# A selective scan on one core: a quarter of the B products of seven groups in twelve go from VectorE to ScalarE and TensorE, and GpSimd works on two units at a time

## The chip, the cores and the metric

The kernel runs on one core of a Trainium2 chip. The metric is device time in microseconds (us). The kernel before took 11069.99 us, the median of three runs (11064.06 to 11072.44).

## What is computed

The input is `x` of 8 x 96 x 64 x 64. A state-space block (layer norm, an in-projection, a depthwise convolution, a selective scan in four directions, a gate, an out-projection), then a convolution block with channel attention, linear attention and a small feed-forward layer with rounded 8-bit weights. The scan matters here. For each of 8 images, 4 directions (`K`) and 192 channels (`d`), with 16 states (`n`) and 4096 places:

```python
def step(h, inp):
    u_t, d_t, b_t, c_t = inp
    dA = jnp.exp(d_t[..., None] * A)
    h = dA * h + (d_t * u_t)[..., None] * b_t[:, :, None, :]
    y = jnp.einsum('bkdn,bkn->bkd', h, c_t)
    return (h, y)
```

So for every channel and state there are a decay `dA`, a product of delta x with B, a first-order recurrence, a product with C, and a sum over states.

## The kernel before

**Units.** Images are taken in pairs `p`. The 192 channels of two images make three tiles `T` of 128 rows: `T` 0 and 1 are the first 128 channels of the one and of the other image, `T` 2 holds the last 64 of both. The 4096 places are cut into four chunks of 1024. A *job* is one (pair, direction, chunk, tile), 192 in all; the tiles of a chunk come in the order 0, 2, 1. A job has four *groups* `j` of 32 channels, and a group four *units* `q`, each of 32 channels x 4 states on 128 partitions x 1024 places. That makes 768 groups and 3072 units.

**The work of a unit.** `spread` (L1299): TensorE copies 32 rows of delta x to all 128 partitions in `pu`, two PSUM banks, by a matmul with a 0/1 matrix, once for a group. `scan` (L1311) handles two units, a *pair*: VectorE multiplies `pu` by the broadcast B rows `bm` into `pb0` and `pb1` (two banks each), then runs the two recurrences (`tensor_tensor_scan`) out of `da` and `pb` into `hc`; GpSimd copies the last column of each unit into `carry` for the next chunk, and multiplies `hc` by the broadcast C rows `cm`. `decay` (L1304): ScalarE makes `da`, the exponential of delta times A, four buffers deep. `total` (L1349): TensorE adds the 4 x 4 states of a group into `yp` with 16 small matmuls; for directions 2 and 3 an identity matmul puts the earlier direction's sum (`prev`) there first, and for direction 2 of all pairs but the first another one (`yet`). ScalarE then copies `yp` to `y`. `hc` has eight buffers (L426), two groups deep.

**Order.** Each engine executes its instructions in the order in which the program records them (`InOrder`, L263 on); nothing overtakes. The main loop (L1400 on) records for every pair: `slots.run()`, `scan`, DMAs for B and C rows, the `decay` of the next pair, at the second pair of group g also `spread(g + 1)` and then `total(g - 1)`, and again `slots.run()`. The ScalarE copy of `yp` is recorded in that last `slots.run()`.

**Background.** Everything else (convolutions, norms, gates, the later layers of earlier pairs, and `steps`, L467, which prepares delta and delta x of the next job) is cut into small pieces, and each `slots.run()` records a few. `Slots` (L283) hands them two PSUM banks, `pg` and the bank of `yp`, and limits them by a budget of TensorE and ScalarE time: it refills by `RATE` and saves up to `CAP`, and each piece pays its estimated time.

Of the kernel before, what the change touches and what calls it, by code (L numbers as in the profile page):

```python
# [25 lines left out]
R = 6  # L26
# [255 lines left out]

class Slots:  # L283
# [7 lines left out]
    RATE, CAP = (2.0, 1.8), (3.0, 2.4)  # L291

    def __init__(self, *banks):
        self.lanes, self.later, self.first, self.at, self.due = [], [], None, 0, {}
        self.banks, self.held, self.big = banks, set(), set()
        self.left, self.behind = [0.0, 0.0], lambda: False
# [3 lines left out]

    def take(self, pe, act, long=0):
        while True:
            i = 1 if self.at % 2 and not long else 0


            due = long and (
                self.at % 4 > (long == 2) or self.at % 16 <= 6 < self.at % 16 + long
            )
            if i not in self.held and not due and min(self.left) > (-2 if long else 0):
                self.held.add(i)  # L310
                self.pay(pe, act)
                return self.banks[i]
            yield
# [7 lines left out]
    def give(self, bank):  # L321
        i = self.banks.index(bank)
        self.after(1, lambda: self.held.remove(i))
# [4 lines left out]
    def run(self):  # L328
        self.at += 1
        self.left = [min(v + r, c) for v, r, c in zip(self.left, self.RATE, self.CAP)]  # L330
        for f in self.due.pop(self.at, ()):
            f()
        if self.first is not None and next(self.first, self) is self:
            self.first = None
        order = [self.lanes, self.later]
        for lanes in order[::-1] if self.behind() else order:
            turn = self.at % len(lanes) if lanes else 0
            for lane in lanes[turn:] + lanes[:turn]:
                if next(lane, self) is self:
                    lanes.remove(lane)  # L340

    def idle(self):
        return not (self.lanes or self.later or self.first or self.due)
# [7 lines left out]
def phase_b(  # L351
# [8 lines left out]
    with ExitStack() as ctx:  # L360
# [28 lines left out]
        gmean = cp.tile([C, C], F32, name="gmean")  # L389
        nc.vector.memset(gmean, 1.0 / (C * 128))  # L390
# [35 lines left out]
        hp = inner.enter_context(tc.tile_pool(name="b_h", bufs=8))  # L426
# [23 lines left out]
        carries, bcs, dus, dls, sts, das, hcs, prevs, yet = ({} for _ in range(9))  # L450
# [11 lines left out]

        def exps():
# [3 lines left out]
        def steps(job):  # L467

            p, k, ci, c, T, at = where(job)
            if T == 0:  # L470

                sts[job // 3] = gp.tile([32 + 2 * R, 512], F32, name="st")
                r0 = 64 + R * (k // 2)
                for i, hs in enumerate(halves):
                    for b in range(2):
                        nc.sync.dma_start(
                            sts[job // 3][32 * i + R * b : 32 * i + R * b + R, :],
                            xd_d[k % 2][2 * p + b][r0 : r0 + R, at][:, hs],
                        )
# [5 lines left out]
            yield  # L485

            while slots.at % 16 != 6:
                yield
            dl = gp.tile([128, CH], F32, name="dls")
            for i, hs in enumerate(halves):  # L490
                bank = slots.banks[i]
                assert i not in slots.held
                slots.held.add(i)
# [11 lines left out]
            nc.sync.dma_start(dl_d[k][p][T][:, at], dl)  # L505
            yield

# [242 lines left out]
        def rest(b, s):  # L750
# [139 lines left out]
            for j in range(8):  # L890
# [17 lines left out]
                h8 = gp.tile([128, 3, 512], F8, name=f"h8{s}")  # L908
# [4 lines left out]
                for i in range(3):  # L913
                    bank = yield from slots.take(0.3, 1.3)
                    pe.matmul(bank, w1q[:, i * 128 : i * 128 + 128], x8, start=True, stop=True)
                    h16 = gp.tile([128, 512], F16, name=f"h16{s}")
# [11 lines left out]
                o16 = gp.tile([128, 512], F16, name=f"h16{s}")[0:C, :]  # L928
# [88 lines left out]
        def before_scans(p):  # L1017
# [26 lines left out]
            def norms(b):  # L1044
# [16 lines left out]
                for j in js:  # L1061
# [16 lines left out]
                    pe.matmul(bank[0:C, 0:4], gmean, cs, start=True, stop=True)  # L1078
                    se.mul(ngm, bank[0:C, 0:4], -1.0)
# [9 lines left out]
                    pe.matmul(bank[0:C, 0:4], gmean, gs, start=True, stop=True)  # L1089
                    se.activation(r, bank[0:C, 0:4], AF.Ln, bias=eps[0:C])  # L1090
# [177 lines left out]
        def weights(u, i):  # L1268
# [6 lines left out]
            if (job // 3, b, q, i) in bcs:  # L1275
                return
            t = bcp.tile([128, CH], F32, name=("bm", "cm")[i], bufs=(4, 5)[i])
            r0 = 32 * (k // 2) + 16 * i + 4 * q
            nc.sync.dma_start(
                t, xd_d[k % 2][2 * p + b][r0 : r0 + 4, at].unsqueeze(0).to_broadcast([32, 4, CH])  # L1280
# [30 lines left out]
        def scan(u):  # L1311
# [3 lines left out]
            step, last = (-1, 0) if k >= 2 else (1, CH - 1)  # L1315
            for i in range(2):
                ve.tensor_mul(pbs[i], pu, bcs[job // 3, batch(u), q + i, 0])
            for i in range(2):
                t = hp.tile([128, CH], F32, name="hc")
                carry = carries[p, k][:, T, 4 * j + q + i : 4 * j + q + i + 1]  # L1320
                ve.tensor_tensor_scan(
                    t[:, ::step], das.pop(u + i)[:, ::step], (pbs[i])[:, ::step],
                    0.0 if ci == 0 else carry, ALU.mult, ALU.add,
                )
                hcs[u + i] = t
            for i in range(2):
                v = u + i
                carry = carries[p, k][:, T, 4 * j + q + i : 4 * j + q + i + 1]
                if ci < NCH - 1:
                    ge.tensor_copy(carry, hcs[v][:, last : last + 1])  # L1330
                ge.tensor_mul(hcs[v], hcs[v], bcs[job // 3, batch(u), q + i, 1])
# [17 lines left out]
        def total(g):  # L1349
# [9 lines left out]
            for n in range(4):  # L1359
                for i in range(4):  # L1360
                    pe.matmul(
                        yp[32 * i : 32 * i + 32, :], add,
                        hcs[4 * g + n][:, 256 * i : 256 * i + 256],
                        start=(n == 0 and k < 2), stop=(n == 3),
                    )
            for n in range(4):
# [33 lines left out]
        for u in range(0, n, 2):  # L1400
# [37 lines left out]
            if q == 2:  # L1438
                if g + 1 < n // 4:
                    spread(g + 1)  # L1440
                if g > 0:
# [505 lines left out]
```

## Time and profile before

| | |
|---|---|
| median of the runs | 11069.99 us |
| the profiled execution, its span | 11058.4 us (the runs are 11.6 us longer at the median) |
| first scan starts, last scan ends | 222 us, 10724 us after the span's start |
| VectorE, GpSimd, TensorE, ScalarE busy | 95%, 82%, 71%, 60% of the span |
| mean granted TensorE clock | 0.815 of full |
| DMA | 1834 MB, 52.8% of 16 engines' span |

The profile is of one execution. "Idle before" a group of instructions is time in which its engine stood still just ahead of them, and the name behind the arrow is what ended it. A float32 matmul appears as two rows, a transpose by the identity as one. `x2` in a timeline merges neighbours of one kind, and its duration is from the start of the first to the end of the last. In names, `pb<-pu,bm` is written and read tiles. Nearly all of the scan's instructions have the line L266, the helper that records them.

### The profile page before, as it was taken

To read this page: it belongs to the slowest core of one execution; us is meant where nothing else is said; L and a number is where in the kernel's file an instruction comes from. 1 tells how busy PE (TensorE), PEld (TensorE's weight loads), DVE (VectorE), ACT (ScalarE), POOL (GpSimd) and SP (SyncE) were. 2 spreads that over 40 slices of the span, in tenths; PEclk is the share of its full clock that TensorE was granted. 3 is DMA by queue.
4 is the path that set the end of the run, shared out by engine and by line. 5 is a ranking of instruction groups with operands and counts; after the bars stand their busy time and mean duration, and the time that the engine had idled before them with its cause. 6 is when DMAs were issued, how large, how long until landed. Compare 5 with 4: busy or idle time off the path is not lost.

```text
span 11058.4 us, 128094 instructions
## 1 busy us (share of the span) xinstructions
PE 7887.2 (71%) x39468; PEld 3111.6 (28%) x39468; DVE 10525.7 (95%) x6651; ACT 6596.3 (60%) x9175; POOL 9028.7 (82%) x6649
## 2 busy tenths in 40 slices
PE   7755778655568887767777787776767776665778
PEld 3322333222223332223222332223322222222223
DVE  4999999999999999999999999999999999999974
ACT  2544765544567666556776656565776656665554
POOL 2788877787898888998888887899889888988860
PEclk8877888877788888878878888887878877777889
DMA  3445554454555555666545555566544555644551
GB/s 117 151 165 180 160 156 157 141 188 156 163 185 172 171 172 157 211 214 195 158 152 160 157 178 159 177 220 209 172 157 159 160 164 179 197 157 140 173 157 37
DMA packets 900188, 1834.20 MB, mean 166 GB/s; under 512 B 247965, under 2 KB 421214, under 8 KB 892462
## 3 DMA queue, kind: packets, MB, share of 16 engines
q1 hardware_dynamic: 899502, 1826.01, 52.8%
q8 instruction: 314, 5.14, 0.2%
q14 instruction: 372, 3.05, 0.1%
HBM read 1405.13 MB, written 420.42 MB: 165 GB/s over the span
## 4 chain that ended last, share of the span: by engine, by line
PE 32%; issue 29%; DVE 17%; POOL 11%; ACT 6%; DMA 4%; SPq 0%; DVEq 0%; POOLq 0%; ACTq 0%
PE pu L266 12%; PE yp L266 11%; DVE hc L266 11%; POOL hc L266 7%; PE pg L266 6%; DVE pb L266 5%; ACT u L266 2%; ACT da L266 2%; POOL u L266 2%; PE t L266 2%; PE ps L197 1%; DMA bm<-xd 1%; POOL turn L266 1%; POOL carry L266 1%; ACT L266 1%
## 5 line engine op out<-in xcount | busy, mean ns | idle before, releaser
L266 POOL TENSOR_TENSOR hc<-hc,cm 128x1024 f32<-128x1024 f32 x3072 | 7230.0, 2359 | 591.0 <-DVE hc L266 382.6
L266 DVE TENSOR_TENSOR_SCAN hc<-da,carry,pb 128x1024 f32<-128x1024 f32 x2304 | 5276.8, 2334 | 38.1 <-ACT da L266 31.5
L266 PE MATMUL pu<-du,c_sel 128*128 128x512 f32 x3072 | 2452.5, 944 | 2244.1 <-DVE pb L266 2239.6
L266 DVE TENSOR_TENSOR pb<-pu,bm 128x1024 f32<-128x1024 f32 x3072 | 3601.6, 1220 | 133.9 <-PE pu L266 105.9
L266 ACT ACTIVATE da<-dl,c_alog 128x1024 f32<-128x1024 f32 x3072 | 3352.8, 1140 | 91.4 <-DVE hc L266 73.8
L266 PEld LDWEIGHTS pu<-du,c_sel 128*128 128x128 f32 x3072 | 790.0, 281 | 3521.1 <-DVE pb L266 2784.8
L266 DVE TENSOR_TENSOR_SCAN hc<-da,pb 128x1024 f32<-128x1024 f32 x768 | 1713.1, 2275 | 38.9 <-ACT da L266 22.8
L266 ACT COPY y<-yp 128x256 f32<-128x256 f32 x768 | 284.4, 370 | 2348.9 <-PE yp L266 2198.4
L266 PE MATMUL yp<-hc,c_add 128*32 128x256 f32 x24576 | 1660.8, 416 | 22.6 <-ACT s L266 6.6
L266 PEld LDWEIGHTS yp<-hc,c_add 128*32 128x32 f32 x24576 | 768.6, 120 | 1200.1 <-issue 628.4
L266 POOL COPY carry<-hc 128x1 f32<-128x1 f32 x2304 | 422.5, 183 | 766.1 <-DVE hc L266 744.9
L266 ACT ACT_TABLE_LOAD x566 | 726.2, 1283 | 38.2 <-DMA cb<-zs 16.9
L266 ACT COPY u<-pg 128x512 f32<-128x512 f32 (+6 forms) x397 | 218.3, 550 | 712.3 <-PE pg L266 641.2
L266 POOL TENSOR_TENSOR u<-u,u 96x512 f32<-96x512 f32 (+1 forms) x426 | 537.5, 1269 | 105.9 <-ACT u L266 101.8
L266 POOL TENSOR_TENSOR du<-du,dls 128x1024 f32<-128x1024 f32 x192 | 452.7, 2358 | 91.5 <-ACT dls L266 91.1
L266 ACT COPY u<-yp 96x512 f32<-96x512 f32 (+6 forms) x347 | 188.0, 542 | 465.5 <-PE yp L266 404.5
L266 PE MATMUL pg<-ain,wmain 96*128 96x512 f32 x792 | 354.1, 599 | 0.0
L266 PE MATMUL pg<-ain,wmix 96*128 96x512 f32 x792 | 353.0, 598 | 0.0
L266 PE MATMUL yp<-prev,ident 128*128 128x256 f32 x768 | 321.9, 512 | 39.0 <-ACT u L266 27.4
L266 PEld LDWEIGHTS yp<-prev,ident 128*128 128x128 f32 x768 | 214.5, 283 | 381.8 <-issue 264.3
L266 PE MATMUL pg<-st,dtw 12*128 12x512 f32 x384 | 218.5, 649 | 49.4 <-ACT u L266 28.8
L266 PE MATMUL yp<-st,dtw 12*128 12x512 f32 x384 | 227.9, 674 | 18.3 <-ACT u L266 10.9
(340 smaller groups left out, 7030.2 us busy)
## 6 DMA issues: line engine op xcount, KB each, us to landing
dl<-dl SPq DMA_DIRECT2D x768, 512.0 KB
bm<-xd SPq DMA_DIRECT2D x512, 512.0 KB
cm<-xd SPq DMA_DIRECT2D x512, 512.0 KB
du<-xi SPq DMA_DIRECT2D x192, 512.0 KB
dl<-dls SPq DMA_DIRECT2D x192, 512.0 KB
ya<-y SPq DMA_DIRECT2D x384, 128.0 KB
prev<-ya SPq DMA_DIRECT2D x384, 128.0 KB
xi<-u SPq DMA_DIRECT2D x152, 256.0 KB
```

What stands on the lines that cost most here:

```text
L197: nc.tensor.matmul(bank[r, :].rearrange("p (h w) -> p h w", w=W), w[:, t if len(which) > 1 or w is wmix else 0, columns], pads[b][:, 8 * j ...
L266: op(*args, **kw)
```

## The change

For the first unit (`q` 0) of a group of tiles 0 and 1, save the first group of tile 0 in each chunk, VectorE's product of `pu` and `bm` is left out. That is 7 of a chunk's 12 groups, called *woven* here. Instead:

- `steps` loads four rows of B more for each image (four more DMAs of 8 KB a chunk), TensorE transposes them (8 transposes a chunk), ScalarE copies them to `bt`.
- `spin`, once for each job of tiles 0 and 1: TensorE transposes delta x (8 blocks of 128 x 128), ScalarE copies them to `dt` (2 copies of 128 x 512), then ScalarE multiplies each of the 8 blocks by each of 4 states' column of `bt`: 32 multiplications of 128 x 128, in four turns of eight, which write every fourth element of `t`. `spin` pays 2.4 for a turn.
- `weave(g + 1)`, recorded between `spread(g + 1)` and `total(g - 1)`: TensorE turns 8 blocks of `t` back into `pb0`.

GpSimd's carry copy and C product take both units of a pair in one instruction (128 x 2 and 128 x 2048), so `hc` becomes four double buffers in place of eight, and `cm` two double buffers in place of five. The budget's `RATE` and `CAP` rise from (2.0, 1.8), (3.0, 2.4) to (2.2, 2.0), (4.0, 4.0); a piece takes whichever of the two banks has rested longer. `dls`, `dt` and `t` share seven buffers; some other tiles share buffers, and a constant is dropped, to make room.

The core of the diff:

```diff
-    RATE, CAP = (2.0, 1.8), (3.0, 2.4)
+    RATE, CAP = (2.2, 2.0), (4.0, 4.0)
...
-            i = 1 if self.at % 2 and not long else 0
...
+            elif min(self.left) > 0:
+                free = [i for i in range(2) if i not in self.held and not (i == 1 and at % 4 == 0)]
+                if free:
+                    i = min(free, key=lambda i: self.used[i])
...
-        hp = inner.enter_context(tc.tile_pool(name="b_h", bufs=8))
+        hp = inner.enter_context(tc.tile_pool(name="b_h", bufs=4))
...
+        def weaves(u):
+            job, j, q = units[u]
+            return q == 0 and woven(job) and not (j == 0 and jobs[job][3] == 0)
...
+        def spin(job):
+            turns[job], b = [], jobs[job][3]
+            bt = bts[job // 3]
+            dt = gp.tile([128, 8, 128], F32, name="turned", bufs=RING)
+            for i in range(2):
+                bank = yield from slots.take(0.6, 0.6)
+                for x in range(4):
+                    pe.transpose(
+                        bank[:, 128 * x : 128 * x + 128],
+                        dus[job][:, 512 * i + 128 * x : 512 * i + 128 * x + 128],
+                        ident,
+                    )
+                se.copy(dt[:, 4 * i : 4 * i + 4, :], bank)
+                slots.give(bank)
+                yield
+            nxt = slots.at
+            while len(turns[job]) < 4:
+                n, at = len(turns[job]), slots.at % 16
+                if slots.at < nxt or (job and woven(job - 1) and n >= EXTRA and 3 < at < 12):
+                    yield
+                    continue
+                nxt = slots.at + 2 - b
+                slots.pay(0.0, 2.4)
+                t = gp.tile([128, 2, 128, 4], F32, name="turned", bufs=RING)
+                for i in range(2):
+                    for m in range(4):
+                        x, c = 2 * n + i, 4 * b + m
+                        se.mul(t[:, i, :, m], dt[:, x, :], bt[:, x, c : c + 1])
+                turns[job].append(t)
+                yield
+        def weave(g):
+            job, j, _ = units[4 * g]
+            for x in range(8):
+                t = turns[job][x // 2][:, x % 2].rearrange("p c n -> p (c n)")
+                pe.transpose(
+                    pbs[0][:, 128 * x : 128 * x + 128], t[:, 128 * j : 128 * j + 128], ident
+                )
...
             for i in range(2):
-                ve.tensor_mul(pbs[i], pu, bcs[job // 3, batch(u), q + i, 0])
+                if not weaves(u + i):
+                    ve.tensor_mul(pbs[i], pu, bcs[job // 3, batch(u), q + i, 0])
             for i in range(2):
...
-            for i in range(2):
-                v = u + i
-                carry = carries[p, k][:, T, 4 * j + q + i : 4 * j + q + i + 1]
-                if ci < NCH - 1:
-                    ge.tensor_copy(carry, hcs[v][:, last : last + 1])
-                ge.tensor_mul(hcs[v], hcs[v], bcs[job // 3, batch(u), q + i, 1])
+            if ci < NCH - 1:
+                ge.tensor_copy(carry, t[:, :, last])
+            ge.tensor_mul(t, t, bcs[job // 3, batch(u), q, 1])
...
                 if g + 1 < n // 4:
                     spread(g + 1)
+                    if weaves(4 * g + 4):
+                        weave(g + 1)
                 if g > 0:
                     total(g - 1)
```

## The prediction

> **What bounds the kernel now.** First the page's busy times and costliest groups:
>
> ```profile
> PE 7887.2 (71%) x39468; PEld 3111.6 (28%) x39468; DVE 10525.7 (95%) x6651; ACT 6596.3 (60%) x9175; POOL 9028.7 (82%) x6649
> ...
> L266 POOL TENSOR_TENSOR hc<-hc,cm 128x1024 f32<-128x1024 f32 x3072 | 7230.0, 2359 | 591.0 <-DVE hc L266 382.6
> L266 DVE TENSOR_TENSOR_SCAN hc<-da,carry,pb 128x1024 f32<-128x1024 f32 x2304 | 5276.8, 2334 | 38.1 <-ACT da L266 31.5
> ...
> L266 DVE TENSOR_TENSOR pb<-pu,bm 128x1024 f32<-128x1024 f32 x3072 | 3601.6, 1220 | 133.9 <-PE pu L266 105.9
> ```
>
> VectorE is busy for 95% of the span; its products and scans hardly wait. So the loop is VectorE's until something else is late. Second, the waits by engine, to see who stands close behind it:
>
> ```profile
> PE pu L266 <- DVE pb L266: 2239.6, 581, 14.5
> ACT y L266 <- PE yp L266: 2198.4, 670, 8.8
> ...
> DVE pb L266 <- PE pu L266: 105.9, 45, 20.4
> ...
> DVE hc L266 <- ACT da L266: 54.3, 43, 5.2
> ```
>
> TensorE comes early to `spread` in 581 of 768 groups, by 3.9 us each (2239.6/581). ScalarE stands at the copy of `yp` until TensorE has summed, 3.3 us each. Both hide their work behind VectorE, but each waits for the other once a group. Third, the timeline of one group and the next (direction 2, where `total` is longest), TensorE's and VectorE's lines:
>
> ```profile
> 5003.50 4.57 DVE L266 TENSOR_TENSOR_SCAN hc<-da,carry,pb 128x1024 f32<-128x1024 f32 x2
> ...
> 5003.65 3.78 PE L266 MATMUL pu<-du,c_sel 128*128 128x512 f32 x4 [2.45 <-DVE pb L266]
> ...
> 5007.99 2.34 DVE L266 TENSOR_TENSOR pb<-pu,bm 128x1024 f32<-128x1024 f32 x2
> ...
> 5008.53 1.93 PE L266 MATMUL yp<-hc,c_add 128*32 128x256 f32 x32
> ...
> 5010.24 4.58 DVE L266 TENSOR_TENSOR_SCAN hc<-da,carry,pb 128x1024 f32<-128x1024 f32 x2
> ...
> 5016.98 4.57 DVE L266 TENSOR_TENSOR_SCAN hc<-da,carry,pb 128x1024 f32<-128x1024 f32 x2
> ...
> 5017.12 1.98 PE L266 MATMUL pu<-du,c_sel 128*128 128x512 f32 x4 [1.19 <-DVE pb L266]
> ...
> 5019.90 1.93 PE L266 MATMUL yp<-hc,c_add 128*32 128x256 f32 x32
> ...
> 5021.47 2.34 DVE L266 TENSOR_TENSOR pb<-pu,bm 128x1024 f32<-128x1024 f32 x2
> ...
> 5023.71 4.58 DVE L266 TENSOR_TENSOR_SCAN hc<-da,carry,pb 128x1024 f32<-128x1024 f32 x2
> ```
>
> A pair takes VectorE 6.74 us (5003.50 to 5010.24), a group 13.48. The same `spread` takes 3.78 us in one group and 1.98 in the next; the mean clock is 0.815. Its rows have 944 ns in the mean, between 590 (fast) and 1222 (slow): (944-590)/(1222-590), some 0.56 of `spread` is slow.
>
> **Part 1: the products removed.** 7 groups of 12, 64 chunks (4 pairs x 4 directions x 4), one product each: 448. Two products take 2.34 us, one 1.22, so the second costs 1.12: 448 x 1.12 = **502 us** off VectorE. The woven group would take 12.36. The scan reads `pb0` from PSUM either way.
>
> **Part 2: what the first scan of a woven group waits for.** It needs `pb0` from `weave`, and an `hc` buffer that `total` of two groups earlier has read: now the first half of the 16 sums, where a single buffer asked for a quarter. `weave` stands ahead of `total` on TensorE. Four transposes take 0.64 us in all and 0.283 each (`pg<-ident,u`, 96 runs), a step of 0.12, so eight take 0.28 + 7 x 0.12 = 1.12 us at full clock; at half clock twice that.
>
> In the slow group, `weave` would run from 5007.43 to 5008.55, the sums start at 5009.65 in place of 5008.53, and their first half ends at 5010.6. VectorE could start at 5009.1, and did start at 5010.24: the gain is gone and 0.4 lost. In the fast group `weave` waits for the scan of `pb0` (5019.25) and ends at 5020.37; half of the sums at 5022.3; VectorE could start at 5022.6 and did at 5023.71: the whole 1.12 is kept. In directions 0 and 1 nothing stands ahead of the sums, which saves the slow case 1.1 us: there some 0.5 is kept. So a slow woven group keeps about 0.05 in the mean.
>
> How many are slow after the change? TensorE's wait ahead of `spread` (3.9 us in 581 groups) loses 1.12 + 1.12, so more groups have a short one; both timeline groups say that 2.45 us of it is slow and 1.19 fast. I take a third slow, half fast and in time, a sixth late (187 of 768 came without a wait; a background piece held them), which keep 0.3: 0.05/3 + 1.12/2 + 0.3/6 = 0.63 of 1.12. Given back: 448 x 0.49 = **220 us** (bounds: 0 when all are fast, 448 x 1.0 = 450 when all are slow).
>
> [...]
>
> **Part 3: ScalarE.** 4096 multiplications of 128 x 128 with a scale per partition. No row has just this: `turn<-turn,dsum` (512 long, a scale) takes 718 ns and `da` (1024) 1140, a slope of 0.824 per element, so 718 - 384 x 0.824 = 402 alone; in a row of equals the next starts 0.09 earlier (two `da` take 2.19), so 0.31. Sum: 1270 us. The 384 copies: 256 x 0.49 + 128 x 0.15 = 145. The instruction order shows 108 more table loads, as background pieces fall differently, x 1.28 = 138. ScalarE goes from 6596 to 8150 us, of 10,860 some 75%. None of it is on VectorE's path by itself; it is queued ahead of `da`, and ahead of the background copies that TensorE waits for. By the rows, ScalarE's work of a group besides `da` and `y` rises from 3.5 to 5.4 us in the mean, in the busiest tenth from 6.4 to 9.0. VectorE waits 54 us for `da` now; I take two and a half times that, **80 us** more (bounds: 0, and 550, the excess over 6.5 us summed over all groups, 6.5 being what a group of 12.4 leaves beside four `da` (4.4), the `y` copy and a wait of a microsecond or so for the sums).
>
> The multiplications write every fourth element. [...] A GpSimd product that reads with a stride takes (855-183)/256 = 2.6 ns an element and a plain one 2.13: a fifth more, though on another engine. No row shows ScalarE so. If an element cost double, 4096 x 0.105 = 430 us more lie on ScalarE; I take none and leave it to the second rival.
>
> **Part 4: GpSimd.** Products of 512 and 1024 elements take 1271 and 2359: 183 fixed. Half of the fixed parts go: 1536 x 0.183 = 281, and 1152 carry copies x 0.183 = 211: 490 us off GpSimd. Not on the path; but a pair's product starts after its second scan, 2.3 us later for the first unit. `total` runs some 8 us later still, so 0; bounds -60 and +100, from the 158 us that TensorE now waits for carries.
>
> **Part 5: the rest, at nothing.** `cm` two pairs deep: the new pair's DMA waits for GpSimd's last use; cover is the other pair, over 6 us; GpSimd waits 20.7 us for `cm` now, bounds 0 and +60. 256 small DMAs (2 MB) more on a queue at 53%: 0, bounds 0 and +20. Behind them on SP stand `dtw` and `du`, due some six slots later. The budget and bank choice move background pieces only: the loop records 3072 `slots.run()` in both, none to wait for background, and the tail after the last scan (334 us) is the same; 0, bounds -50 and +50. TensorE gains 1536 transposes of delta x and B beside those of `weave`, 0.2 ms, in its waits.
>
> **The sum.** -502 + 220 + 80 = -202. 11058.4 - 202 = 10856 for the span; the median stands 11.6 above it: **10868 us**, 1.8% faster. By its own terms this case runs from 10,720 to 10,990.
>
> **Rivals.**
>
> - *The cover holds.* TensorE, busier, is nearly always fast and in time, so given back is some 50: 11070 - 502 + 50 = 10,618. For it: 1.98 behind the short wait. Against: directions 2 and 3, and 187 late groups already.
> - *ScalarE becomes the bound, and the kernel is slower.* Turns stand in ScalarE's queue between two pairs' `da`, at up to two turns (5 us) a pair for tile 1; when a group holds over 6.5 us, `da` is late, TensorE's next piece too, and the next `y`. With the whole excess: -502 + 220 + 550 = +268, 11,338. It decides for slower from 282 us of waits for `da`. For it: 75% busy with a wait for TensorE in each group. Against: the four `da` buffers let an excess be made up a pair later, and turns of tile 1 fall mostly in the groups of tile 2, which are not woven.
> - *Nothing comes of it.* `weave` and the sums end where the product ended, in every woven group: -502 + 450 + 50: 11,070. For it: 0.56 slow now. Against: the shorter waits.
>
> **Chances.** Forecast 0.43, cover 0.24, ScalarE 0.25, nothing 0.08. About 0.2% is what a measurement of this kernel can tell from no change. Faster by more 0.67, within 0.08, slower 0.25. The range reaches into both outer cases: 10,600 to 11,230.
>
> **What would show it.** Products of VectorE: 2624 in place of 3072, and `hc` waits for `yp` (now under 20 us) become the largest wait of VectorE, near 220. `spread`'s rows get faster than 944 ns in the mean. A turn of eight takes 2.5 us; over 3.3 would say that the stride costs. GpSimd's rows read 1536 at 4.5 us. Waits for `da` at 130; over 280 and the second rival is there. The forecast is wrong if the waits for `pu` rise beyond 250, which would say that TensorE is late as a whole.

## The result and the profile after

The changed kernel takes 11,802.1 us (median of 4 runs, 11,785 to 11,808); the kernel before took 11,070.0 beside it. The ratio is 1.066, with an interval of 1.0644 to 1.0674: 732 us slower, where 202 us faster was forecast.

The page of the changed kernel, its busy times and the rows that answer to those shown of before:

```profile
PE 8636.7 (73%) x44588; PEld 3778.0 (32%) x44588; DVE 10119.3 (86%) x6202; ACT 8068.3 (68%) x13763; POOL 8648.0 (73%) x3961
...
L266 POOL TENSOR_TENSOR hc<-hc,cm 128x2048 f32<-128x2048 f32 x1536 | 6973.1, 4540 | 765.8 <-DVE hc L266 500.8
L266 DVE TENSOR_TENSOR_SCAN hc<-da,carry,pb 128x1024 f32<-128x1024 f32 x2304 | 5275.2, 2331 | 452.1 <-PE yp L266 255.7
L266 DVE TENSOR_TENSOR pb<-pu,bm 128x1024 f32<-128x1024 f32 x2624 | 3098.1, 1218 | 734.1 <-PE pu L266 679.0
...
L266 ACT ACTIVATE turned<-turned,bt 128x128 f32<-128x128 f32 x4096 | 1305.4, 503 | 0.3
...
L266 PE MATMUL yp<-st,dtw 12*128 12x512 f32 x384 | 322.4, 932 | 390.7 <-ACT u L266 343.1
```

The work did get less: VectorE's products fell from 3601.6 to 3098.1 us, its busy time by 406. But it is busy for 86% in place of 95%, so it now stands and waits. The last scan ends at 11,462 us in place of 10,724, and the tail behind it is nearly as long as before: the time is lost in the loop. The last row is the second half of the delta product in `steps`: TensorE stands 390.7 us ahead of it, mostly for ScalarE's `u`; it was 18.3 us before:

```profile
L266 PE MATMUL yp<-st,dtw 12*128 12x512 f32 x384 | 227.9, 674 | 18.3 <-ACT u L266 10.9
```

VectorE's waits and TensorE's in the changed kernel (total, times, longest):

```profile
DVE pb L266 <- PE pu L266: 679.0, 224, 10.1
DVE hc L266 <- PE yp L266: 353.5, 322, 2.5
DVE hc L266 <- ACT da L266: 250.9, 178, 9.8
```

```profile
PE pu L266 <- DVE pb L266: 1722.2, 405, 15.4
PE yp L266 <- ACT u L266: 519.8, 229, 7.4
PE pg L266 <- ACT u L266: 426.7, 314, 9.6
```

VectorE's three waits were 105.9, 19 and 54.3 us; they are 1283 now. TensorE's cover ahead of `spread` shrank from 2239.6 us in 581 groups to 1722.2 in 405, and its waits for ScalarE's `u` rose from these in the kernel before:

```profile
PE yp L266 <- ACT u L266: 292.3, 184, 7.2
...
PE pg L266 <- ACT u L266: 121.8, 118, 6.4
```

Summed by place, 451 of the 679 us for `pu` stand at one group of the four, the third of a job (148 us in tile 0, 125 in tile 2, 178 in tile 1); before it was under 1. Tile 2 is not woven, so this part isn't the weave's.

One such place, in the timeline of the changed kernel (second group of a job of tile 0 and the one that follows; TensorE, VectorE, ScalarE):

```profile
1244.87 1.12 PE L266 MATMUL pg<-st,dtw 12*128 12x512 f32 x2
1246.11 1.68 PE L266 MATMUL yp<-u,mean 96*96 96x512 f32 x2
1252.18 2.07 PE L266 MATMUL yp<-st,dtw 12*128 12x512 f32 x2 [4.39 <-ACT u L266]
1254.18 3.78 PE L266 MATMUL pu<-du,c_sel 128*128 128x512 f32 x4
```

```profile
1247.86 4.58 DVE L266 TENSOR_TENSOR_SCAN hc<-da,carry,pb 128x1024 f32<-128x1024 f32 x2
1257.99 1.23 DVE L266 TENSOR_TENSOR pb<-pu,bm 128x1024 f32<-128x1024 f32 x1 [5.56 <-PE pu L266]
```

```profile
1248.15 1.28 ACT L266 ACT_TABLE_LOAD   x1
1249.44 0.69 ACT L266 ACTIVATE turned<-pg,c_dtb 128x512 f32<-128x512 f32 x1
1250.15 1.28 ACT L266 ACT_TABLE_LOAD   x1
1251.44 0.68 ACT L266 ACTIVATE u<-yp,eps 96x512 f32<-96x512 f32 x1
```

A background piece (`u,mean`) took the bank of `yp` between the two halves of the delta product. Its ScalarE half (`u<-yp,eps`) stands behind a table load, the first half's softplus and another table load, and ends at 1252.12. Only then may the second half write `yp`, at 1252.18; `spread` stands behind it on TensorE, and VectorE, ready at 1252.44, gets `pu` at 1257.99. One small piece at the wrong place, and VectorE stood for 5.56 us.

### The profile page after: what moved, and what is told of

Same layout as the page of the kernel before. It is cut to its first block, busy times and chain, and to the rows that moved or that the text cites. A ratio compares the mean times of both kernels' runs of the same rounds, so it can differ in the third digit from the quotient of the medians.

```text
span 11806.4 us, 137459 instructions
## 1 busy us (share of the span) xinstructions
PE 8636.7 (73%) x44588; PEld 3778.0 (32%) x44588; DVE 10119.3 (86%) x6202; ACT 8068.3 (68%) x13763; POOL 8648.0 (73%) x3961
## 5 line engine op out<-in xcount | busy, mean ns | idle before, releaser
L266 POOL TENSOR_TENSOR hc<-hc,cm 128x2048 f32<-128x2048 f32 x1536 | 6973.1, 4540 | 765.8 <-DVE hc L266 500.8
L266 DVE TENSOR_TENSOR pb<-pu,bm 128x1024 f32<-128x1024 f32 x2624 | 3098.1, 1218 | 734.1 <-PE pu L266 679.0
L266 PE MATMUL pu<-du,c_sel 128*128 128x512 f32 x3072 | 2425.0, 934 | 1722.8 <-DVE pb L266 1722.2
L266 PE MATMUL yp<-hc,c_add 128*32 128x256 f32 x24576 | 1556.5, 396 | 5.0 <-ACT u L266 3.2
L266 POOL COPY carry<-hc 128x2 f32<-128x2 f32 x1152 | 215.7, 187 | 1498.0 <-DVE hc L266 1420.0
L266 ACT ACTIVATE turned<-turned,bt 128x128 f32<-128x128 f32 x4096 | 1305.4, 503 | 0.3
L266 ACT ACT_TABLE_LOAD x674 | 864.7, 1283 | 29.8 <-DMA cb<-zs 17.9
L266 PEld LDWEIGHTS pb<-ident,turned 128*128 128x128 f32 x3584 | 572.0, 180 | 473.1 <-issue 281.7
L266 POOL TENSOR_TENSOR du<-du,turned 128x1024 f32<-128x1024 f32 x192 | 452.7, 2358 | 294.8 <-ACT turned L266 269.5
L266 PE MATMUL pb<-ident,turned 128*128 128x128 f32 x3584 | 615.6, 329 | 31.3 <-DVE hc L266 29.5
L266 PE MATMUL yp<-st,dtw 12*128 12x512 f32 x384 | 322.4, 932 | 390.7 <-ACT u L266 343.1
L266 ACT COPY u<-pg 128x512 f32<-128x512 f32 (+5 forms) x420 | 232.0, 552 | 452.6 <-PE pg L266 402.3
L266 ACT COPY u<-yp 96x512 f32<-96x512 f32 (+5 forms) x324 | 177.4, 548 | 283.4 <-PE yp L266 190.2
```

What stands on the lines that cost most here:

```text
L266: op(*args, **kw)
```

## The experiments

The first theory: that piece, let in by the planner's new rules, is the main loss. The rival: ScalarE's turns, or `weave` itself.

**The two halves of the delta product in one step**, so that no piece can come between:

```diff
                 if i:
                     exps()
-                else:
-                    yield
```

> Both halves of the next job's delta product are recorded in one step, the two matmuls and the two softplus one behind the other, so that no background piece comes between them. Theory 1 (the order at this step: the second half shares its bank with a piece whose ScalarE copy is queued behind a table load and a softplus, and spread of the third group stands behind it on TensorE): VectorE's wait for pu at the third group of a job falls from 451 us to under 100, the whole wait for pu from 679 to about 300, the time to 11,350-11,450. Theory 2 (ScalarE simply has too much work, and any place will do for TensorE to wait): the wait for pu moves to other groups, the time stays at 11,700-11,800.

Measured: 11,564 us, ratio 1.045. TensorE's idle time ahead of `yp<-st,dtw` fell from 390.7 to 10.7 us, the waits for `pu` at the third group from 451 to 226. The time fell by 238, less than expected: other pieces now queue in `pg` behind ScalarE's softplus (`turned`; 339.6 us, 50.6 in the changed kernel).

**Nothing woven** (`woven` returns False: no turns, no `weave`; planner, pairs and B transposes stay):

```diff
-            return jobs[job][3] < 2
+            return False
```

> No group is woven (VectorE makes all B products again; the B rows are still transposed); GpSimd's pairs, the two-bank choice and the budget stay as changed. Theory 1 (order at the delta step): the third group still waits for pu, about half as much since ScalarE is less late; 11,200-11,350. Theory 2 (ScalarE's work): 11,050-11,120, the time of the kernel before.

Measured: 11,552 us, ratio 1.044. Neither number was right. What is left of the change when nothing is woven costs 484 us, and TensorE's idle time ahead of `yp<-st,dtw` is still 275.4 us.

**The pairs on GpSimd alone**, put into the kernel before (double `hc` and `cm` buffers, one product and one carry copy for two units):

```diff
-                ge.tensor_mul(hcs[v], hcs[v], bcs[job // 3, batch(u), q + i, 1])
+            ge.tensor_mul(t, t, bcs[job // 3, batch(u), q, 1])
```

> The kernel before with GpSimd's carries and C products for two units at once, hc in four double and cm in two double buffers, and nothing else changed. As predicted this is worth nothing: 11,040-11,100, with GpSimd's busy time about 490 us lower. A rival: the product that starts one scan later, or hc that is freed in halves, costs over 100 us by itself: 11,170 or more.

Measured: 11,082 us, ratio 1.0015 [1.0005, 1.0024], 14 us, though GpSimd's busy time fell by 405 us (490 expected).

**Lighter turns**: eight multiplications of 128 become two of 512, which leave out three of the four states' columns of B.

```diff
-                    for m in range(4):
-                        x, c = 2 * n + i, 4 * b + m
-                        se.mul(t[:, i, :, m], dt[:, x, :], bt[:, x, c : c + 1])
+                    x, c = 2 * n + i, 4 * b
+                    se.mul(t[:, i], dt[:, x, :].unsqueeze(2).to_broadcast([128, 128, 4]),
+                           bt[:, x, c : c + 1])
```

> The changed kernel with each turn's eight multiplications of 128 made by two of 512 (all four states take the first state's column of B, which leaves that part of the computation wrong): ScalarE has about 700 us less to do, all transposes stay. Theory 1 (order at the delta step): 100-200 us faster, 11,600-11,700, the third group's wait for pu mostly stays. Theory 2 (ScalarE's work): the waits for da and pu fall to near those of before, 11,150-11,350.

Measured: 11,710 us, ratio 1.058. The turns' row fell by half, from 1305.4 to 675.7 us, and bought 92 us, near theory 1's 100 to 200; the waits for `pu` stayed (697 us). That speaks against ScalarE's total as the limit, though half of the turns is still there.

**Each edit of the planner alone**, in the kernel before: first the budget, then the choice of bank (`take`, `hold` and `used` as in the change's diff).

```diff
-    RATE, CAP = (2.0, 1.8), (3.0, 2.4)
+    RATE, CAP = (2.2, 2.0), (4.0, 4.0)
```

> The kernel before with the higher budget (RATE 2.2, 2.0 and CAP 4.0, 4.0) and nothing else. The run without woven groups has shown that pairs, budget and bank choice cost 484 us together, the pairs alone 14. Theory 1 (the bank choice lets a piece stand between the halves of the delta product): the budget costs little, 11,070-11,150. Theory 2 (a higher budget puts more background into one step, ScalarE and TensorE come late in bursts): 11,300 or more.

> The kernel before with the new choice of bank for a background piece (whichever has rested longer, in any step but one of four) and the old budget. Theory 1 (bank choice): 11,300-11,500, with the wait for pu at the third group near 300 us. Theory 2 (budget): under 11,150.

Measured: 11,095 us (1.0019 [1.0009, 1.0028]) and 11,212 us (1.0125 [1.011, 1.014]); the third group's wait is near 0 in both. Alone they cost 26 and 142 us; the second lies between the two theories' times. With the banks alone TensorE's wait for `u` in `pg` is already 332 us (121.8 before).

**Both together**, in the kernel before, and nothing else:

> The kernel before with two edits of the planner together, the new budget and the new choice of bank, and nothing else. Alone they cost 26 and 142 us. Theory (the two edits act together: the larger ScalarE allowance leaves budget in the step between the halves of the delta product, and the new choice of bank lets a background piece use it): about 11,450 to 11,550, VectorE's waits for pu near 450, about 300 of them at the third group of a job, and TensorE's delta product waits about 270 us for ScalarE. Rival (the costs add up, and the other 300 us of the kernel without weaving come from its shared buffers or its B transposes): about 11,240, third-group waits near 0.

Measured: 11,461 us, ratio 1.035 [1.034, 1.037]. The two cost 392 us, 224 more than their sum. The waits of VectorE and the row of the delta product's second half:

```profile
DVE pb L266 <- PE pu L266: 459.2, 147, 19.9
```

```profile
L266 PE MATMUL yp<-st,dtw 12*128 12x512 f32 x384 | 278.3, 812 | 244.8 <-ACT u L266 171.1 <-ACT h L266 53.6 <-ACT small L266 15.3
```

273 of the 459 us stand at the third group, and the delta product waits 244.8. The theory is right: neither edit alone opens the gap, and the two together do. With the old `CAP` the delta product's payment (2.5 of at most 2.4) leaves no budget in its step; with 4.0 it leaves up to 1.5. And the old rule offers in each of the two steps only the bank that the delta product holds, where the new one gives out the other.

**Both together, no piece in steps 6 and 7**:

```diff
-            elif min(self.left) > 0:
+            elif at not in (6, 7) and min(self.left) > 0:
```

> The same kernel with both planner edits, but no background piece takes a bank in steps 6 and 7 of a job, the steps of the delta product. Theory: the third-group waits go (near 0), the time falls back to about 11,200 to 11,260, the sum of the edits alone. Rival (the background that is kept out waits elsewhere, as in the woven kernel): within 60 us of the kernel with both edits.

Measured: 11,300 us, ratio 1.021. The third group's wait is under 1 us and the idle time ahead of the delta product 16.8; 161 us came back, and the time is 40 us above the theory's range. 231 remain: VectorE still waits 244 us for `pu` (106 before), and TensorE 344.0 us for `u` in `pg`, as with the new choice of bank alone.

**The same in the changed kernel** (with the new pieces unpaid, so that they keep their dates), and then with `total(g - 1)` recorded ahead of `spread` too:

```diff
+            elif at not in (6, 7) and min(self.left) > (-9 if pe == 0 else 0):
...
-                bank = yield from slots.take(0.6, 0.6)
+                bank = yield from slots.take(0.0, 0.0)
...
-                slots.pay(0.0, 2.4)
```

```diff
             if q == 2:
+                if g > 0:
+                    total(g - 1)
                 if g + 1 < n // 4:
                     spread(g + 1)
...
-                if g > 0:
-                    total(g - 1)
```

> The changed kernel, woven, with no background piece that takes a bank in the two steps of the delta product (steps 6 and 7 of 16), and the pieces of the change (transposes, turns) not charged to the budget, as the background would miss its dates otherwise. Theory 1 (what stands between the delta product and the third group's spread): its wait for pu falls from 451 us to under 60, time 11,200-11,350; the waits for yp (hc buffers) stay near 340. Theory 2 (ScalarE has too much work, wherever it stands): 11,600 or more.

> As the run before it, and total of the last group is recorded ahead of spread and weave, where TensorE otherwise waits for VectorE. If the waits for yp come from weave standing ahead of total, they fall from about 340 us to under 60, and spread's slow share falls; 10,850-11,050, faster than both kernels. The rival: GpSimd's product for two units is not ready then, TensorE waits for it with spread behind, and the wait for pu grows by more than is won: 11,250 or more.

Measured: 11,682 us (1.055) and 12,002 us (1.084). Both miss their theory's time by hundreds of microseconds and meet the rival's. In the first the third group's waits went, but others were there: `pu` 428, `yp` 335, `da` 377 (251 in the changed kernel). In the second the wait for `yp` went too, and `spread`, now behind the sums, was late everywhere: `pu` 1447. There TensorE waits in `yp` for GpSimd's products, as the rival had it (347 us), and longer for ScalarE's softplus and copies (773 us). So something besides the planner stands in the woven kernel.

**Turns without weave**: the changed kernel with all of ScalarE's turns and the transposes of delta x, but VectorE makes all products.

```diff
-            return q == 0 and woven(job) and not (j == 0 and jobs[job][3] == 0)
+            return False
```

> The changed kernel with all of its turns on ScalarE and its transposes of delta x, but weave is left out and VectorE makes all products as before, so the turned tiles are read by nobody. Theory (VectorE's waits for an hc buffer come from weave's place ahead of the sums; waits for da come from the turns): waits for yp under 40 us in place of 354, waits for da stay near 200, and the time about 11,800 to 11,950, which is 11,552 (nothing woven) plus the cost of the turns, 250 to 400. Rival (the waits for hc buffers come from ScalarE's turns delaying what TensorE stands behind): waits for yp stay over 200 us.

Measured: 11,700 us, ratio 1.057; waits for `yp` 19, for `da` 168. The wait for the `hc` buffer is `weave`'s, as the theory had it. The turns and the transposes of delta x cost 148 us, less than expected. And the step from here to the changed kernel, which takes 504 us of products off VectorE, makes it 102 us slower.

**Weave alone on the old planner**: the kernel before with the pairs, and `weave` in the 448 groups, of a constant.

```diff
+        def weave(g):
+            for x in range(8):
+                pe.transpose(pbs[0][:, 128 * x : 128 * x + 128], sel[:, x % 4, :], ident)
...
+                if not weaves(u + i):
+                    ve.tensor_mul(pbs[i], pu, bcs[job // 3, batch(u), q + i, 0])
...
                     spread(g + 1)
+                    if weaves(4 * g + 4):
+                        weave(g + 1)
```

> The kernel before with its own planner (old budget, old choice of bank), pairs on GpSimd, and weave alone: in the same 448 groups the first unit's product is left out and TensorE's eight transposes take its place, but of a constant, so ScalarE and the background have nothing to do for it (the first unit's B product is not computed there). Theory (the planner is what made the change slow; weave on an undisturbed TensorE keeps about half of the 502 us): 10,780 to 10,900, waits for yp 200 to 350, waits for pu near 110, by the prediction's own terms -502 and +220. Rival (weave gives all of it back wherever it stands, as the step from the kernel with turns alone to the changed one suggests, which was +102): 11,050 to 11,200, waits for pu and yp together over 500.

Measured: 11,037 us, ratio 0.9968 [0.9956, 0.9979]. Both theories missed: the planner is as before, and yet `weave` keeps only 34 us, 45 against the pairs alone. Its waits and a slow woven group in its timeline (TensorE, then VectorE):

```profile
DVE hc L266 <- PE yp L266: 316.8, 290, 8.7
...
DVE pb L266 <- PE pu L266: 98.2, 62, 6.7
```

```profile
5923.55 3.78 PE L266 MATMUL pu<-du,c_sel 128*128 128x512 f32 x4 [2.67 <-DVE pb L266]
5927.12 1.91 PE L266 MATMUL pb<-ident,c_sel 128*128 128x128 f32 x8
5928.97 2.10 PE L266 MATMUL yp<-hc,c_add 128*32 128x256 f32 x32
```

```profile
5923.40 4.58 DVE L266 TENSOR_TENSOR_SCAN hc<-da,carry,pb 128x1024 f32<-128x1024 f32 x2
5928.08 1.23 DVE L266 TENSOR_TENSOR pb<-pu,bm 128x1024 f32<-128x1024 f32 x1
5930.38 2.35 DVE L266 TENSOR_TENSOR_SCAN hc<-da,carry,pb 128x1024 f32<-128x1024 f32 x1 [1.06 <-ACT da L266]
```

`spread` is slow (3.78 us), `weave` behind it is slow too (1.91, not 1.12), half of the sums ends at 5930.20, and the scan starts at 5930.38: 2.40 us after the last one ended (5927.98), where the kernel before takes 2.16 with two products (5021.55 to 5023.71 in its timeline). The record names `da`, which ends at 5930.26: in this group it was as late as the sums. That is rare. `spread` was slow, taking over 2.9 us, in 296 of the 448 woven groups; in 242 of these the first scan waits for the sums (261 us of the 317), in 13 for `da`. The median of this stretch between two groups' scans is 1.25 us where `spread` was fast, but 2.1 (directions 0 and 1) and 2.5 (2 and 3) where it was slow. In the mean it is 1.73 and 2.42, where the kernel with the pairs alone takes 2.33 and 2.37 in the same groups: what is kept comes from the fast third.

**Weave and the turns on the old planner**: eight multiplications, once a group, ahead of the first pair.

```diff
             slots.run()
+            if q == 0 and job < len(jobs) and woven(job):
+                for i in range(2):
+                    for m in range(4):
+                        se.mul(tt[:, i, :, m], sel[:, m, :], dsum[:, i : i + 1])
             scan(u)
```

> The kernel just described with ScalarE's multiplications too: a turn of eight once a group, ahead of the first pair's product, in each of the four groups before a woven tile (508 turns; they read and write tiles that nothing else needs). Theory (ScalarE has room for them when the background keeps its places): within 100 us of the kernel with weave alone, by the prediction's +80, and waits for da under 200. Rival (ScalarE's queue is the limit as soon as turns stand in it): 250 to 500 us slower than with weave alone, waits for da over 280.

Measured: 11,342 us, ratio 1.025: 305 us more, and the waits for `da` went from 91 to 376. The rival is right: with a block of 2.57 us (8 x 1305.5/4064) ahead of the decays VectorE waits for `da` 306 times, in spite of its four buffers.

**Weave in the second pair**, where neither `spread` nor the sums that free `hc` stand beside it:

```diff
-            return q == 0 and woven(job) and not (j == 0 and jobs[job][3] == 0)
+            return q == 2 and woven(job) and not (j == 0 and jobs[job][3] == 0)
...
+            if weaves(u + 2 - q):
+                if q == 0:
+                    weave(g)
             if q == 2:
                 if g + 1 < n // 4:
                     spread(g + 1)
-                    if weaves(4 * g + 4):
-                        weave(g + 1)
```

> The kernel with weave alone on the old planner, but weave stands in the second pair of the same 448 groups (it is recorded behind the first pair's scans, not between spread and total), so the third unit's product is left out. There neither spread nor the sums that free the hc buffer stand beside it. Theory (weave alone gained only 34 us because TensorE is already at its limit between VectorE's last product of a group and the next group's first scan): most of 502 us is kept, 10,600 to 10,750, waits for yp near 30. Rival (the group's step is set elsewhere, for example by GpSimd's 78% or by TensorE as a whole, so time does not fall wherever weave stands): within 60 us of 11,037.

Measured: 10,764 us, ratio 0.972 [0.971, 0.974], 14 us above the theory's range; waits for `yp` 40. By its place alone `weave` is worth 308 us in place of 34. A woven group of it (TensorE, then VectorE):

```profile
5756.68 1.98 PE L266 MATMUL pu<-du,c_sel 128*128 128x512 f32 x4 [0.94 <-DVE pb L266]
...
5765.66 1.09 PE L266 MATMUL pb<-ident,c_sel 128*128 128x128 f32 x8 [1.08 <-DVE hc L266]
```

```profile
5756.54 4.57 DVE L266 TENSOR_TENSOR_SCAN hc<-da,carry,pb 128x1024 f32<-128x1024 f32 x2
...
5763.28 4.57 DVE L266 TENSOR_TENSOR_SCAN hc<-da,carry,pb 128x1024 f32<-128x1024 f32 x2
5767.88 1.23 DVE L266 TENSOR_TENSOR pb<-pu,bm 128x1024 f32<-128x1024 f32 x1
5769.02 2.34 DVE L266 TENSOR_TENSOR_SCAN hc<-da,carry,pb 128x1024 f32<-128x1024 f32 x1
```

`weave` starts when the pair's first scan has read `pb0` (5765.66) and is done 1 us before the second scan ends; the third unit's scan follows the product without a wait. From one second pair's first scan (5756.54) to the next (5769.02) it is 12.48 us, where a group of the kernel before takes 13.48: 1.00 of the 1.12 is kept.

**That and the turns**, four multiplications behind the decays of each pair:

```diff
+            if job < len(jobs) and woven(job):
+                for m in range(4):
+                    se.mul(tt[:, q // 2, :, m], sel[:, m, :], dsum[:, 0:1])
```

> The kernel just described with ScalarE's 4064 multiplications, four at a time behind the decays of each pair in place of eight at once ahead of the first pair (their results are read by nobody). Theory (ScalarE has room if no long block stands ahead of the decays): within 120 us of the kernel without them, waits for da under 200. Rival (any extra 1.28 us a pair on ScalarE holds up da and the y copies, as with eight at once): 250 to 400 us slower than without them, which would leave about 11,000.

Measured: 10,907 us, ratio 0.985; waits for `da` 148. The same multiplications cost 143 us here, 23 above the theory's bound, and 305 in blocks of eight ahead of a pair (where `weave` stood at its old place too, so part of the difference may be that).

**Whole kernels on this ground.** The arithmetic of the change, on the old planner, with `weave` in the second pair. The transposes take the bank that the planner doesn't use in the step, and up to k multiplications (`turn(k)`) stand behind the decays of a pair:

```diff
+    def spare(self):
+        while True:
+            i = 0 if self.at % 2 else 1
+            if i not in self.held and (i == 0 or self.at % 4 == 2) and self.at % 16 not in (6, 7):
+                self.held.add(i)
+                return self.banks[i]
+            yield
...
-                bank = yield from slots.take(0.6, 0.6)
+                bank = yield from slots.spare()
...
+            if q == 0 and weaves(u + 2):
+                weave(g)
+            turn(6)
```

> A whole kernel on what the runs showed: the old planner, pairs on GpSimd, weave in the second pair, for the groups 1 to 3 of tiles 0 and 1 (384 products). The transposes of B and of delta x take the bank that the planner doesn't use in that step, behind all pieces, and the 32 multiplications of a job stand up to six at a time behind the decays of each pair. Theory (place, not totals): 384/448 of the 319 us that the weave in the second pair kept is 273; ScalarE's multiplications cost 143 to 200, transposes and copies up to 60: 11,000 to 11,060, faster than before by 10 to 70. Rival (transposes of delta x in the planner's free bank hold up TensorE as the background pieces in steps 6 and 7 did): 11,150 to 11,300, waits for pu over 250.

> The same with the change's own 448 groups' count: group 0 of tile 1 too, and up to eight multiplications behind the decays of a pair (2.56 us), so that they are done in time. Theory: 64 products more keep up to 45 us, the longer blocks on ScalarE cost up to 100 more: 10,980 to 11,110. Rival (a block of eight on ScalarE costs as with the turns ahead of the first pair, +305): 11,120 to 11,200, waits for da over 280.

Measured: 11,254 us (1.0165) and 11,189 us (1.011 [1.009, 1.013]). The theory's numbers were missed in both, the first by some 200 us. The rivals' times were met; in the first with the rival's sign (402 us of waits for `pu`), in the second without it (152 us for `da`). The second is 613 us faster than the changed kernel, and 115 slower than before. From the kernel with `weave` and turns in these places (10,907) it differs by the transposes of delta x and B, their copies and buffers, by blocks of up to eight multiplications in place of four, and by `weave` reading what was turned: 282 us. VectorE's waits for `pu` are 416 us, 122 of them at the fourth group of tile 2, just behind the two halves of the transposes; TensorE waits 235 us in `yp` for ScalarE's `turned`, 195 of them for its copies of the transposes. Keeping the halves apart:

```diff
-            if i not in self.held and (i == 0 or self.at % 4 == 2) and self.at % 16 not in (6, 7):
+            if i not in self.held and (i == 0 or self.at % 4 == 2) and (
+                self.at % 4 != 3 or self.at % 16 == 15) and self.at % 16 not in (6, 7):
...
-                yield
+                yield from wait(2)
```

> The whole kernel with 448 groups, but the two halves of the delta x transposes no longer stand in one group: the step just ahead of spread is left out for them (save the last step of a job), and at least two steps lie between the halves. Theory (the 140 and 130 us of waits for pu at the fourth group of tile 2 and the first and fourth of tile 1 come from both halves, their copies and a block of turns in one group): waits for pu fall from 416 to 200 to 280, and the time to 11,000 to 11,080. Rival (each half costs its 1 to 2 us wherever it stands, since TensorE has nothing free in any group): within 50 us of 11,189, the waits only spread over more groups.

Measured: 11,200 us, ratio 1.012. The waits for `pu` fell to 311 us, but those for `weave` (`PE pb`) rose from 97 to 154 and for `da` from 152 to 174. The rival is right: the time is what it was, the waits have only moved. No whole kernel here beats the kernel before, and which part of the 282 us the transposes themselves cost stays open.

## Why the prediction was wrong, point by point

The chain of kernels splits the 732 us. Each number is a difference of medians, and depends on the order, since the parts act on each other. The forecast stands beside it:

| step | time | difference | forecast |
|---|---|---|---|
| before | 11,069 | | |
| both edits of the planner | 11,461 | +392 | 0 |
| + pairs, B transposes, shared buffers (nothing woven) | 11,552 | +91 | 0 |
| + the turns on ScalarE, delta x transposes | 11,700 | +148 | +80 |
| + `weave`, 448 products fewer (the changed kernel) | 11,802 | +102 | -502 + 220 |

Off the forecast by 392, 91, 68 and 384, these parts make up, but for rounding, the 934 us between -202 and +732.

- **The step that failed first** is in part 5: "The budget and bank choice move background pieces only: ... 0, bounds -50 and +50". They cost 392 us. That no `slots.run()` waits for background was true, and beside the point: what counted is which piece stood between two others in TensorE's queue (5.56 us of VectorE's time at the place shown). The place between the delta product's halves had been kept free by a budget that happened to be too small and by a bank rule that offered only the bank in use, and the prediction didn't ask what kept it so. It had a sign of it in hand: the 108 more table loads that it counted, "as background pieces fall differently", are of pieces that now stand there. With both edits alone there are 611 loads in place of 566, and 566 again as soon as no piece stands between the halves. Shown for the third group by the pair of edits (273 us) and by clearing the steps (161 back). The 231 us that stay are only in part explained: TensorE waits 344 us for `u` in `pg`, which the new choice of bank alone brings as well; that this causes them was not tried by itself, and stays open. Nor were the 91 us of the next step taken apart.
- **Part 2**, "I take a third slow", failed as well, and in the chain by as much: +102 where -282 was forecast. The mechanism was right (`weave` pushes back the sums that free `hc`), and its size was wrong. In the kernel with weave alone two thirds of the spreads stay slow (0.66 take over 2.9 us; 0.71 before, where the prediction read 0.56 out of a mean). There a slow `spread` had a slow `weave` behind it (1.53 us in the mean, up to 1.91; 1.18 behind a fast one), but the prediction, which had said "at half clock twice that", put 1.12 into its slow group. So nearly all is given back: 502 - 45 = 457, at the upper bound of 450, where 220 was taken. "`weave` and the sums end where the product ended", the last rival, is what weave does there; it had a chance of 0.08. The two groups of the timeline had misled it. In the kernel before, `spread` was slow in all 253 groups with over 4 us of wait ahead of it and in 0.76 of those with 2 to 3 us, but also in 0.54 of those with 1 to 2 us and in 0.35 of those without a wait: with a shorter wait the slow `spread` was rarer there, and not gone. The wait for `hc` as a price, 317 us in that kernel and 354 in the changed one (19 before), was the right thing to watch.
- **Part 2's clock.** The prediction's estimate for eight transposes was 1.12 us at full clock and twice that at half. In the changed kernel `weave`'s eight take 1.04 us at a granted clock of 1.00 and 1.91 at 0.50 (medians of 193 and 57 woven groups; the others lie across a change of the clock). In the kernel before, `spread` was slow in 547 groups, at a granted clock of 0.50, and fast in 221, at 1.00 (medians); and ahead of the loop the clock went from 0.50 to 1.00 behind 16 transposes with nothing between them on TensorE (the last section has the lines). What the slow spreads go with in the traces is the wait ahead of them, by the shares in the point above.
- **Part 3**, +80 for a later `da`: the turns cost 148 us in the changed kernel's company, 305 in blocks ahead of a pair and 143 in halves behind the decays. The waits for `da` were forecast at 130 and measured 251; the rival's condition, 282, was not met in the changed kernel, but was by 376 in the kernel with blocks. "Slower" had a chance of 0.25 for this rival's sake; that it came true for other reasons is luck. ScalarE's busy time, 8068 us, was forecast to 1%.
- **Part 1** was right: 503.5 us off the products, by rows. **Part 4** too: a pair takes 4540 ns, and the pairs cost 14 us in all, though GpSimd's busy time fell by 405 us there and not 490. A multiplication with every fourth element written takes 1305.4/4096 = 0.319 us (0.31 forecast), so no cost of the stride shows. Table loads rose by 108 as counted.
- The test, "the waits for `pu` rise beyond 250, which would say that TensorE is late as a whole", caught the failure (679), though its reading was too broad: 451 of them stand at one group of four.

## What to carry to other kernels

A planner's budget and its bank rule keep places free that nobody wrote down: when one is loosened, look on each engine for what now stands between two dependent instructions (here the two halves of the delta product: 273 us of waits at the third group, under 1 with the steps cleared). Work taken off the busiest engine was worth here only what the next engine could follow at that very place: the same product, handed to the same eight transposes, was worth 34 us between `spread` and the sums and 308 us half a group later. When parts of a change are tried alone, try the pairs of them too: 26 and 142 made 392.

## What the runs showed of the hardware that was not expected

- Queued neighbours on VectorE overlapped by some 0.09 us in the record of the kernel before (the median of 6316; a scan ends at 5003.50 + 4.57 = 5008.07 in the kernel before, the next product starts at 5007.99), so 448 products of 1.22 us are worth 1.12 each. In the changed kernel, where VectorE waits more, 4923 neighbours overlap, and VectorE's busy time fell by 406 us where the products' row fell by 503.5.
- The granted TensorE clock went from 0.50 to 1.00 behind 16 transposes. In the kernel before, ahead of the loop, they (`ps<-ident,xn` and `xt`) stand by themselves on TensorE from 178.03 to 181.47 us, at a granted clock of 0.50 and some 1.06 us for four; from 181.49 the clock is 1.00, and four take 0.60 us:

```profile
178.03 1.09 PE L157 MATMUL ps<-ident,xn 128*96 128x128 f32 x4 [0.47 <-DVE xn L145]
178.91 1.06 PE L169 MATMUL ps<-ident,xt 128*96 128x128 f32 x4
179.76 1.06 PE L157 MATMUL ps<-ident,xn 128*96 128x128 f32 x4
180.62 1.03 PE L169 MATMUL ps<-ident,xt 128*96 128x128 f32 x4
181.47 0.61 PE L157 MATMUL ps<-ident,xn 128*96 128x128 f32 x4
181.92 0.60 PE L169 MATMUL ps<-ident,xt 128*96 128x128 f32 x4
```

- The mean granted clock was 0.815 before and 0.843 in the kernel with weave in the second pair, where the share of slow spreads fell to 0.54. The two did not go together in these runs: with the sums ahead of `spread` the share was 0.23 at a mean clock of 0.806.
